# A four-layer convolution and attention network: the gating pass reordered with its norm folded in, and the convolution's scales moved by 0/1 products

## The chip, the cores and the metric

The kernel runs on one core of one Trainium2 chip. The metric is the device time of one execution in microseconds; the kernel before takes 4220.08 us, the median of three runs (4215.15 to 4225.31). Everything is computed in float32.

The profile names the engines so: PE is TensorE (matrix products; PEld its loads of the stationary operand), DVE is VectorE, ACT is ScalarE, POOL is GpSimd, SP is SyncE, which here only issues transfers. Names that end in q are the engines' instruction queues.

## The reference, cut to what matters

The input is x of shape (8, 384, 32, 32). Four layers follow, each with a group norm ahead of it and a residual around it. The change concerns the seam inside layer 0 and the beginning of layer 1.

```python
x = x + L0(gn(x)); x = x + L1(gn(x)); x = x + L2(gn(x)); x = x + L3(gn(x))

def L0(x):        # for each of q, k, v: depthwise 3x3, batch norm over all 8 images, gelu, 1x1
    y = depthwise3x3(x, dw)
    y = gelu((y - mean(y)) * rsqrt(var(y) + 1e-5) * g + b)     # mean, var over images and pixels
    q = einsum('oc,bchw->bohw', pw, y)                         # likewise k, v
    out = softmax(q k^T * scale) v                             # 8 heads of 48
    return batch_norm(einsum('oc,bchw->bohw', w_out, out))

def L1(x):        # 4 experts, the 2 best of each pixel
    scores = softmax(x_flat @ gate_w + gate_b)
    top_v, top_i = top_k(scores, 2); top_w = softmax(top_v)
    present[k, e] = does any pixel of all images choose expert e as its k-th
    coef = einsum('ke,kbhw->ebhw', present, top_w)             # every expert runs on every pixel
    return sum over e of coef[e] * (w2[e] @ relu(w1[e] @ x + b1[e]) + b2[e])

def L2(x):        # depthwise 3x3 and 1x1 with weights rounded to -1, 0, 1 and a scale
def L3(x):        # attention with sampled keys
```

Two things force a barrier over all images: the batch norm of layer 0 needs the statistics of all 8 images before the first Gelu, and `present` needs the routing of all 8 images before the first expert's result.

## The kernel before

An image lies in SBUF as 128 partitions of 3 channels each: `x[b].rearrange("(p c) n -> p c n", c=3)`, so a chunk `c` is 128 x 1024. Layer 0's convolution runs on TensorE in groups of 42 channels (nine groups and a rest of six channels), for q, k and v at once; its results go to the DRAM tensors `raw[v]`, and VectorE takes statistics:

```python
raw = [dram.tile([B, C, N], F32, name=f"raw{v}") for v in range(3)]
work = [(b, g) for b in range(B) for g in range(NGC + 1)]       # the rest group is g = NGC = 9
for n, (b, g) in enumerate(work):
    ...                                                        # matmuls into pk[0], pk[1]
                nc.scalar.copy(y[:, hs], pk[h][: 3 * nch, :])
                nc.vector.bn_stats(cst[: 3 * nch, g, 2 * b + h, :], y[:, hs])
    for v in range(3):
        nc.scalar.dma_start(out=raw[v][b, g * GC : g * GC + nch, :], in_=y[v * nch : (v + 1) * nch, :])

scs, shs = bn_params(cst, NGC + 1, gb0[:, 0, :], gb0[:, 1, :], "qkv")
ssd = dram.tile([2, 3, C], F32, name="ssd")
for k, t in enumerate((scs, shs)):                              # 12 small stores ...
    for v in range(3):
        nc.sync.dma_start(out=ssd[k, v, : NGC * GC]..., in_=t[v * GC : (v + 1) * GC, :NGC])
        nc.scalar.dma_start(out=ssd[k, v, NGC * GC :]..., in_=t[v * GR : (v + 1) * GR, NGC : NGC + 1])
for k, t in enumerate((sc0, sh0)):                              # ... and 6 loads
    for v in range(3):
        nc.sync.dma_start(out=t[:, v * KC : (v + 1) * KC], in_=ssd[k, v].rearrange("(c p) -> p c", p=P))
```

The scales `scs` and shifts `shs` are made in the partitions of the convolution groups and are wanted in the partitions of the activations `g`, which are loaded again from `raw`. Gelu applies them, then the projections run:

```python
nc.scalar.activation(g[:, c, :], g[:, c, :], AF.Gelu, bias=sh0[:, j : j + 1], scale=sc0[:, j : j + 1])
...
load_b(0); gelu_b(0)                                            # gelu_b goes over v in (2, 0, 1)
for v in range(2):
    for h in range(2):
        project(0, 0, v, h)                                     # pq <- w_in[v], g
```

Attention ends with `out_project` (`po`), whose result goes to `o_dram`; a check of the sums decides whether a slower branch runs. It doesn't run here. Then comes what prepares layer 1, in this order:

```python
gw, gbias, ewt = load_w("gw"), load_w("gbias"), load_w("ewt")
w1, b1, w2, b2 = (load_w(n) for n in ("w1", "b1", "w2", "b2"))
...                                                             # dw2, pw2: ternary weights of layer 2, 35 DVE steps
wq3, wk3, wv3, wp3 = (load_w(n) for n in ("wq3", "wk3", "wv3", "wp3"))
...                                                             # small weights of layer 3
xc = pc.enter_context(tc.tile_pool(name="c_x", bufs=2))
for b in range(B):
    load_image(xt, x_img[b]); load_image(ot, o_dram[b])
    for c in range(KC):
        nc.scalar.activation(ot[:, c, :], ot[:, c, :], AF.Identity, bias=..., scale=...)
        nc.vector.tensor_tensor(xt[:, c, :], xt[:, c, :], ot[:, c, :], ALU.add)
        nc.sync.dma_start(out=x1_dram[b][:, c, :], in_=xt[:, c, :])
    ss = gn_stats(xt, f"c{b}", pool=wd)                         # scale and shift of the group norm
    for c in range(KC):
        affine(h1[:, c, :], xt[:, c, :], ss)
    for t in range(NT8):                                        # 8 x 3 matmuls: pixels x experts
        for c in range(KC):
            nc.tensor.matmul(pg[:, t * NE : (t + 1) * NE], lhsT=h1[:, c, t * P : (t + 1) * P],
                             rhs=gw[:, c, :], start=(c == 0), stop=(c == KC - 1))
    ...                                                         # lg = pg + bias; softmax, top 2, pres, wk
```

`gn_stats` is six `bn_stats`, an aggregate, two small matmuls with copies between them (sums over the partitions of a group) and a power on GpSimd. After the loop a matmul joins `pres` over the partitions, and layer 1 proper begins: `layer1(pl, b)` loads `x1_dram[b]` again, normalises it and runs the experts (`ph`, `y`) with results of three PSUM banks. From then on the units of layer 1 of image b+1 are mixed with layers 2 and 3 of image b.

Of the kernel before, what the change touches and what calls it, by code (L numbers as in the profile page):

```python
# [40 lines left out]
def tile_kernel(ctx: ExitStack, tc: tile.TileContext, i: dict, out: bass.AP):  # L41
# [108 lines left out]
    def ternary(dst, w, shape, scale_ap):  # L150

        if isinstance(scale_ap, list):
            for c, s in enumerate(scale_ap):
                nc.vector.tensor_scalar(dst[:, c, :], w[:, c, :], s, RNE, ALU.mult, ALU.add)
        else:
            nc.vector.tensor_scalar(dst, w, scale_ap, RNE, ALU.mult, ALU.add)
        nc.vector.tensor_scalar(dst, dst, RNE, 1.0, ALU.subtract, ALU.min)
        nc.vector.tensor_scalar(dst, dst, -1.0, None, ALU.max)
        nc.vector.tensor_tensor(dst, dst, w, ALU.subtract)
        nc.vector.tensor_tensor(dst, w, dst, ALU.add)  # L160
# [10 lines left out]
    raw = [dram.tile([B, C, N], F32, name=f"raw{v}") for v in range(3)]  # L171
    sc0 = const.tile([P, 9], F32, name="sc0")
    sh0 = const.tile([P, 9], F32, name="sh0")
    with ExitStack() as pa:
# [27 lines left out]
        gb0 = load_a("gb0")  # L202

# [36 lines left out]
        work = [(b, g) for b in range(B) for g in range(NGC + 1)]  # L240
# [7 lines left out]
        for n, (b, g) in enumerate(work):  # L248
            if n + AHEAD < len(work):
                b2, g2 = work[n + AHEAD]  # L250
                if g2 == 0:
                    norm(b2)
                    if b2 + 1 < B:
                        load_x(b2 + 1)
# [24 lines left out]
            for v in range(3):  # L279
                nc.scalar.dma_start(  # L280
                    out=raw[v][b, g * GC : g * GC + nch, :], in_=y[v * nch : (v + 1) * nch, :]
                )

        scs, shs = bn_params(cst, NGC + 1, gb0[:, 0, :], gb0[:, 1, :], "qkv")
        ssd = dram.tile([2, 3, C], F32, name="ssd")
        for k, t in enumerate((scs, shs)):
            for v in range(3):
                nc.sync.dma_start(
                    out=ssd[k, v, : NGC * GC].rearrange("(g c) -> c g", c=GC),
                    in_=t[v * GC : (v + 1) * GC, :NGC],  # L290
                )
                nc.scalar.dma_start(
                    out=ssd[k, v, NGC * GC :].rearrange("(c g) -> c g", g=1),
                    in_=t[v * GR : (v + 1) * GR, NGC : NGC + 1],
                )
        for k, t in enumerate((sc0, sh0)):
            for v in range(3):
                nc.sync.dma_start(
                    out=t[:, v * KC : (v + 1) * KC],
                    in_=ssd[k, v].rearrange("(c p) -> p c", p=P),  # L300
                )
# [28 lines left out]
    def gelu_image(g, v):  # L330
        for c in range(KC):
            j = v * KC + c
            nc.scalar.activation(  # L333
                g[:, c, :], g[:, c, :], AF.Gelu,
                bias=sh0[:, j : j + 1], scale=sc0[:, j : j + 1],
            )

    with ExitStack() as pb:
# [26 lines left out]
        def load_b(b):  # L365
            acts[b] = []
            for v in range(3):
                g = gp.tile([P, KC, N], F32, tag=f"g{v}", name=f"g{v}_{b}", bufs=2 if v < 2 else 1)
                load_image(g, raw[v][b].rearrange("(c p) n -> p c n", p=P))
                acts[b].append(g)  # L370

        def gelu_b(b):
            for v in (2, 0, 1):
                gelu_image(acts[b][v], v)
# [173 lines left out]
    with tc.If(redo > 0):  # L548
        with ExitStack() as pb:
# [13 lines left out]
            with tc.For_i(0, B) as bi:  # L563
                act = []
                for v in range(3):
                    g = gp.tile([P, KC, N], F32, tag=f"g{v}", name=f"g{v}_e")
                    nc.sync.dma_start(
                        out=g, in_=raw[v][bass.ds(bi, 1)].rearrange("o (c p) n -> p (o c) n", p=P)
# [112 lines left out]
    def load_w(name, pool=wd):  # L681
        src = i[name]
        t = pool.tile(list(src.shape), F32, tag=name, name=name + "_sb")
# [4 lines left out]
    w1, b1, w2, b2 = (load_w(n) for n in ("w1", "b1", "w2", "b2"))  # L688


    tap2 = wd.tile([P, KC, 9], F32, name="tap2")
    upw2 = wd.tile([P, KC, C], F32, name="upw2")
    m2 = wd.tile([P, KC], F32, name="m2")
    s2 = wd.tile([P, KC], F32, name="s2")
    with tc.tile_pool(name="w2_raw", bufs=1) as wr:
        dw2 = load_w("dw2", wr)
        pw2 = load_w("pw2", wr)
        nc.vector.tensor_reduce(m2, dw2, AX.X, ALU.add, apply_absolute_value=True)
        nc.vector.tensor_scalar(m2, m2, 1.0 / 9.0, 1e-5, ALU.mult, ALU.max)
        nc.vector.reciprocal(s2, m2)  # L700
        ternary(tap2, dw2, None, [s2[:, c : c + 1] for c in range(KC)])
        nc.vector.reciprocal(m2, s2)
        for c in range(KC):
            nc.vector.tensor_scalar(tap2[:, c, :], tap2[:, c, :], m2[:, c : c + 1], None, ALU.mult)
        mp = wd.tile([P, 1], F32, name="mp")
        sp = wd.tile([P, 1], F32, name="sp")
        nc.vector.tensor_reduce(mp, pw2, AX.XY, ALU.add, apply_absolute_value=True)
        pm = bank("pm")
        nc.tensor.matmul(pm[:, 0:1], lhsT=ones, rhs=mp, start=True, stop=True)
        nc.vector.tensor_scalar(mp, pm[:, 0:1], 1.0 / (C * C), 1e-5, ALU.mult, ALU.max)  # L710
        nc.vector.reciprocal(sp, mp)
        ternary(upw2, pw2, None, sp)
        nc.vector.reciprocal(mp, sp)


    wq3, wk3, wv3, wp3 = (load_w(n) for n in ("wq3", "wk3", "wv3", "wp3"))
    pb3, dw3, bn3, pw3 = (load_w(n) for n in ("pb3", "dw3", "bn3", "pw3"))
    ref3, npos = load_w("ref3"), load_w("npos")
    so3 = wd.tile([P, 1], F32, name="so3")
    bo3 = wd.tile([P, 1], F32, name="bo3")  # L720

    nc.vector.tensor_scalar(bo3, bn3[:, 4:5], 1e-6, None, ALU.add)
    rsqrt(so3, bo3, 1)
    nc.vector.tensor_tensor(so3, so3, bn3[:, 1:2], ALU.mult)
    nc.vector.tensor_tensor(bo3, bn3[:, 0:1], bn3[:, 3:4], ALU.subtract)
    nc.vector.scalar_tensor_tensor(bo3, bo3, so3, bn3[:, 2:3], ALU.mult, ALU.add)

    x1_dram = [dram.tile([P, KC, N], F32, name=f"x1_{b}") for b in range(B)]
    wk = wd.tile([P, B, 2, NT8], F32, name="wk")
    pres = wd.tile([P, 2, NE], F32, name="pres")
    nc.vector.memset(pres, 0.0)
    ss1 = []

    def bc(ap):
        return ap.unsqueeze(2).to_broadcast([P, NT8, NE])

    with ExitStack() as pc:  # L740
        xc = pc.enter_context(tc.tile_pool(name="c_x", bufs=2))
        tcp = pc.enter_context(tc.tile_pool(name="c_t", bufs=2))
        ew_b = ewt.unsqueeze(1).to_broadcast([P, NT8, NE])
        for b in range(B):
            xt = xc.tile([P, KC, N], F32, tag="x", name=f"xc{b}")
            load_image(xt, x_img[b])
            ot = xc.tile([P, KC, N], F32, tag="o", name=f"oc{b}")
            load_image(ot, o_dram[b])
            for c in range(KC):
# [5 lines left out]
                nc.sync.dma_start(out=x1_dram[b][:, c, :], in_=xt[:, c, :])  # L755
            ss = gn_stats(xt, f"c{b}", pool=wd)
            ss1.append(ss)
            h1 = xc.tile([P, KC, N], F32, tag="h", name=f"hc{b}")
            for c in range(KC):
                affine(h1[:, c, :], xt[:, c, :], ss)  # L760
            pg = bank(f"pg{b}")
            for t in range(NT8):
                for c in range(KC):
                    nc.tensor.matmul(
                        pg[:, t * NE : (t + 1) * NE],
                        lhsT=h1[:, c, t * P : (t + 1) * P],
                        rhs=gw[:, c, :],
                        start=(c == 0),
                        stop=(c == KC - 1),
                    )  # L770

            def tt(name):
                return tcp.tile([P, NT8, NE], F32, tag=name, name=f"{name}_{b}")

            def tv(name):
                return tcp.tile([P, NT8], F32, tag=name, name=f"{name}_{b}")

            lg, e, sc, eq, oh = tt("lg"), tt("e"), tt("sc"), tt("eq"), tt("oh")
            m, d = tv("m"), tv("d")
            nc.vector.tensor_tensor(  # L780
                lg, pg[:, : NT8 * NE].rearrange("p (t e) -> p t e", e=NE),
                gbias.unsqueeze(1).to_broadcast([P, NT8, NE]), ALU.add,
            )
            nc.vector.reduce_max(m, lg, AX.X)
            nc.vector.tensor_tensor(lg, lg, bc(m), ALU.subtract)
            nc.scalar.activation(e, lg, AF.Exp)
            nc.vector.reduce_sum(m, e, AX.X)
            nc.vector.reciprocal(m, m)
            nc.vector.tensor_tensor(sc, e, bc(m), ALU.mult)
            tops = []  # L790
            for k in range(2):
                mk, ek, hit = tv(f"m{k}"), tv(f"e{k}"), tcp.tile(
                    [P, NE], F32, tag=f"hit{k}", name=f"hit{k}_{b}"
                )
# [3 lines left out]
                nc.vector.tensor_tensor(eq, eq, ew_b, ALU.mult)  # L798
# [7 lines left out]
            nc.vector.tensor_tensor(d, tops[1], tops[0], ALU.subtract)  # L806
            nc.scalar.activation(d, d, AF.Exp)
            nc.vector.tensor_scalar(m, d, 1.0, None, ALU.add)
            nc.vector.reciprocal(wk[:, b, 0, :], m)
            nc.vector.tensor_tensor(wk[:, b, 1, :], d, wk[:, b, 0, :], ALU.mult)  # L810
# [17 lines left out]
    for k, t in enumerate((dp, p1)):  # L828
        nc.vector.tensor_tensor(ybt, b2, t.unsqueeze(1).to_broadcast([P, KC, NE]), ALU.mult)
        nc.vector.reduce_sum(yb[:, k, :], ybt, AX.X)  # L830

# [38 lines left out]
    def layer1(pl, b):  # L870
# [5 lines left out]
        def enter(h):  # L876
# [6 lines left out]
            for t in range(4):  # L883
                w0 = wk[:, b, 0, 4 * h + t : 4 * h + t + 1].to_broadcast([P, P])
                nc.tensor.matmul(
                    pw[:, t * P : (t + 1) * P], lhsT=w0, rhs=ident, start=True, stop=True
# [368 lines left out]
    with ExitStack() as pd:  # L1255
        pl = Pools(pd, "d", 5)
        for u in layer1(pl, 0):
            u()
        for b in range(B):
# [57 lines left out]
def _layouts(a):  # L1317
# [33 lines left out]

    hrow = np.arange(C).reshape(NH0, HD0)
# [6 lines left out]
    for n in "qk":  # L1359
        L[f"w{n}0"] = _chunks(a[f"L0_conv_pw_{n}"].T[order][:, rows])  # L1360
# [56 lines left out]
```

## Time and profile before

| what | value |
|---|---|
| median of 3 runs | 4220.08 us (4215.15 to 4225.31) |
| span of the profiled run | 4222.7 us |
| PE, share of the span | 3887.0 us, 92% |
| DVE | 1624.3 us, 38% |
| ACT | 1512.2 us, 36% |
| POOL | 261.5 us, 6% |
| moved by DMA | 238.60 MB, mean 57 GB/s |

The profile is of one execution. The page gives the busy time of each engine, the span in 40 equal slices, the costliest groups of instructions and the transfers. Further views answer for a stretch of time: busy times in given stretches, who waited for whom, and the instructions in order of time. In a line of a group, the words are the line of the program, the engine, the operation, output and inputs by the program's names, the shape, the count, busy time and mean, then the idle time ahead of it and what ended that. Ends of matmuls are modelled, so a busy PE is not PE at its peak; and the page's share of busy time is a mean over stages that have different limits.

### The profile page before, as it was taken

What the parts mean: (1) busy time and instruction counts of PE and PEld (TensorE: products, weight loads), DVE (VectorE), ACT (ScalarE), POOL (GpSimd) and SP (SyncE); (2) the same over time, 40 slices, a digit from 0 to 9 for tenths busy, and PEclk for the clock granted to TensorE, in tenths of its full rate; (3) what the DMA queues carried; (4) which work ended last, traced back from release to release, by engine and by line L of the source; (5) the groups of instructions that cost most, each with busy time, mean ns of one, the idle gap of its engine ahead of it and who ended that gap; (6) DMA issues with size and microseconds to landing.
All of it is one profiled execution on the core that took longest, in us unless ns stands there. A gap on an engine that the chain in (4) does not pass through costs nothing.

```text
span 4222.7 us, 31867 instructions
## 1 busy us (share of the span) xinstructions
PE 3887.0 (92%) x11992; PEld 1647.5 (39%) x11992; DVE 1624.3 (38%) x2807; ACT 1512.2 (36%) x1683; POOL 261.5 (6%) x157
## 2 busy tenths in 40 slices
PE   7999699999999999999347999999999999999957
PEld 3444233333333333333244444444445354444423
DVE  3333111121211111221343373836465655737364
ACT  2222364546364554334122223232423232232313
POOL 0000000000000000000000002020201111020202
PEclk9999899999999999999557999999999999999978
DMA  6776411111111010000542000000000000000000
GB/s 200 216 214 199 130 50 29 43 37 50 30 44 54 22 50 24 18 19 10 219 179 85 0 16 30 15 15 30 15 30 15 15 15 30 15 30 15 1 30 16
DMA packets 81554, 238.60 MB, mean 57 GB/s; under 512 B 20830, under 2 KB 21214, under 8 KB 81006
## 3 DMA queue, kind: packets, MB, share of 16 engines
q1 hardware_dynamic: 68932, 198.67, 14.4%
q10 hardware_dynamic: 12456, 37.76, 2.9%
q8 instruction: 99, 1.62, 0.2%
q14 instruction: 67, 0.55, 0.0%
HBM read 100.50 MB, written 88.09 MB: 45 GB/s over the span
## 4 chain that ended last, share of the span: by engine, by line


## 5 line engine op out<-in xcount | busy, mean ns | idle before, releaser
L458 ACT ACTIVATE p<-s 128x1024 f32<-128x1024 f32 x512 | 497.6, 1021 | 653.2 <-PE s L451 652.5
L923 PE MATMUL y<-hd,w_sb 128*128 128x512 f32 x1152 | 523.7, 598 | 0.0
L903 PE MATMUL ph<-h,w_sb 128*128 128x512 f32 x1152 | 503.0, 595 | 0.0
L464 PE MATMUL pav<-p,vt 128*64 128x512 f32 x2048 | 499.2, 608 | 0.0
L451 PE MATMUL s<-qk,qk 48*128 48x512 f32 x1536 | 383.8, 618 | 22.2 <-ACT p L458 22.2
L271 PE MATMUL pk<-st,cw_sb 126*126 126x496 f32 (+1 forms) x864 | 383.2, 606 | 0.8 <-DVE ve_a L111 0.8
L903 PEld LDWEIGHTS ph<-h,w_sb 128*128 128x128 f32 x1152 | 217.9, 191 | 262.9 <-issue 257.5
L923 PEld LDWEIGHTS y<-hd,w_sb 128*128 128x128 f32 x1152 | 212.0, 190 | 260.4 <-issue 248.5
L464 PEld LDWEIGHTS pav<-p,vt 128*64 128x64 f32 x2048 | 124.8, 136 | 342.7 <-issue 334.1
L271 PEld LDWEIGHTS pk<-st,cw_sb 126*126 126x126 f32 x864 | 167.6, 196 | 211.7 <-issue 205.0
L431 DVE STREAM_TRANSPOSE tu<-pav 128x512 f32<-128x512 f32 x64 | 45.9, 717 | 503.5 <-PE pav L464 503.5
L973 DVE SCALAR_TENSOR_TENSOR y<-h,tap,y 128x961 f32<-128x961 f32 (+1 forms) x192 | 231.8, 1232 | 1.8
L1053 DVE SCALAR_TENSOR_TENSOR off<-q,dw_sb,off 128x240 f32<-128x240 f32 (+2 forms) x576 | 230.2, 459 | 2.6
L913 ACT ACTIVATE hd<-ph,b_sb 128x512 f32<-128x512 f32 x192 | 131.2, 683 | 278.4 <-PE ph L903 278.2
L451 PEld LDWEIGHTS s<-qk,qk 48*128 48x128 f32 x1536 | 131.2, 186 | 253.6 <-issue 173.2
L278 DVE BATCH_NORM_STATS2 cst<-y 126x6 f32<-126x512 f32 (+1 forms) x160 | 109.0, 690 | 252.2 <-ACT y L277 252.1
L277 ACT COPY y<-pk 126x512 f32<-126x512 f32 (+1 forms) x160 | 92.9, 584 | 287.5 <-PE pk L271 192.8
L914 DVE TENSOR_TENSOR hd<-hd,cb 128x512 f32<-128x512 f32 x192 | 132.1, 688 | 118.6 <-ACT hd L913 118.2
L400 PE MATMUL pq<-g,wq_sb 128*128 128x512 f32 x288 | 138.4, 617 | 34.3 <-ACT g L333 34.3
L126 ACT ACTIVATE h<-x,ss_d 128x1024 f32<-128x1024 f32 x48 | 56.8, 1231 | 298.3 <-DVE ss_d L114 298.3
L984 PE MATMUL pw<-y,upw 128*128 128x512 f32 x288 | 132.3, 615 | 31.2 <-DVE y L973 31.2
L1143 ACT ACTIVATE p<-s 128x1024 f32<-128x1024 f32 x96 | 93.6, 1020 | 173.0 <-PE s L1136 172.9
(218 smaller groups left out, 4113.3 us busy)
## 6 DMA issues: line engine op xcount, KB each, us to landing
g<-raw SPq DMA_DIRECT2D x72, 512.0 KB
st<-pad SPq DMA_DIRECT2D x216, 168.0 KB
raw<-y ACTq DMA_DIRECT2D x216, 168.0 KB
x<-x SPq DMA_DIRECT2D x48, 512.0 KB
xa<-in_x_dram SPq DMA_DIRECT2D x24, 512.0 KB
o<-ot SPq DMA_DIRECT2D x48, 256.0 KB
xc<-in_x_dram SPq DMA_DIRECT2D x24, 512.0 KB
oc<-o SPq DMA_DIRECT2D x24, 512.0 KB
```

The costliest lines, as they stand in the source:

```text
L271: nc.tensor.matmul(pk[h].rearrange("p (h w) -> p h w", w=W)[: 3 * nch, :, o0 : o0 + c1 - c0], lhsT=lhs, rhs=rhs, start=(k == 0), stop=(k = ...
L400: nc.tensor.matmul(pq, lhsT=w_in[v][:, c, pr * P : (pr + 1) * P], rhs=acts[b][v][:, c, h * HALF : (h + 1) * HALF], start=(c == 0), stop=(c ...
L451: nc.tensor.matmul(s[:, j * HALF : (j + 1) * HALF], lhsT=kt[r, kc * P : (kc + 1) * P], rhs=qt[r, h * HALF : (h + 1) * HALF], start=True, s ...
L458: nc.scalar.activation(p, s, AF.Exp, scale=scale)
L464: nc.tensor.matmul(pav[64 * j : 64 * j + 64, :], lhsT=vts[b % 2][:, kc, 2 * hd : 2 * hd + 2, :].rearrange("p a b -> p (a b)"), rhs=p[:, j ...
L903: nc.tensor.matmul(ph, lhsT=w1[:, e, c, dc * P : (dc + 1) * P], rhs=state["h1"][:, c, :], start=(c == 0), stop=(c == KC - 1),)
L913: nc.scalar.activation(hd, ph, AF.Relu, bias=b1[:, k : k + 1])
L914: nc.vector.tensor_tensor(hd, hd, state["cb"], ALU.mult)
L923: nc.tensor.matmul(y, lhsT=w2[:, e, dc, m * P : (m + 1) * P], rhs=state[k], start=(k == 0), stop=(k == NE * KC - 1),)
L973: nc.vector.scalar_tensor_tensor(d, src[:, r0 + dy : r1 + dy, c0 + dx : c1 + dx], tap2[:, c, t : t + 1], d, ALU.mult, ALU.add,)
L984: nc.tensor.matmul(pw[:, hs], lhsT=upw2[:, c, m * P : (m + 1) * P], rhs=y[:, c, hs], start=(c == 0), stop=(c == KC - 1),)
L1053: nc.vector.scalar_tensor_tensor(d, f, dw3[:, t : t + 1], d, ALU.mult, ALU.add)
```

## The change

It joins two changes that stand side by side.

The first concerns the gating pass. Images are loaded ahead of the weights, in four buffers and not two, and the group norm in front of the gate is folded into the gate's weights: with scale a and shift s per channel, `gate_w . (a x + s)` is `(a gate_w) . x + s . gate_w`. So the normalised image is not made; the gate weights are the stationary operand and the image streams past them, 512 pixels at a time; the logits come out with experts in the partitions and are transposed back by four small matmuls. Routing runs twice (after images 0 to 5 and 6, 7) and not once an image. The x1 stores are issued by ScalarE's queue. The ternary weights of layer 2 are prepared later, within layer 1 of image 0 (`weights23`).

The second concerns the scales of the convolution. `raw` is laid out as the images are, so that a channel's partition is given by three blocks of 42 and a rest of two, and the scales reach it through products with 0/1 matrices (`sel0`, `sel1`) and a mask, with no trip to DRAM. The rest group comes first in each image. Gelu goes over q, k, v, and the rows of the projection weights follow the new channel order.

```diff
-    raw = [dram.tile([B, C, N], F32, name=f"raw{v}") for v in range(3)]
+    raw = [dram.tile([B, P, KC, N], F32, name=f"raw{v}") for v in range(3)]
-        work = [(b, g) for b in range(B) for g in range(NGC + 1)]
+        work = [(b, g) for b in range(B) for g in (NGC, *range(NGC))]
 ...
-        ssd = dram.tile([2, 3, C], F32, name="ssd")
-        (12 stores to ssd, 6 loads from it)
+        nc.vector.tensor_copy(both[:, 0, :], scs)
+        nc.vector.tensor_copy(both[:, 1, :], shs)
+        nc.vector.tensor_tensor(rest, both[: 3 * GR, :, NGC:]..., one3..., ALU.mult)
+        for v in range(3):
+            nc.tensor.matmul(pm[:, 0, v, : 2 * (NGC + 1)], lhsT=sel0[:, v, :], rhs=both..., ...)
+            nc.tensor.matmul(pm[:, 1, v, : 2 * KC], lhsT=sel1[:, v, :], rhs=rest..., ...)
+        for v in range(3):
+            nc.vector.tensor_tensor(got[:, v], pm[:, 0, v, ...]..., msk..., ALU.mult)
+        nc.vector.reduce_sum(ss0..., got..., AX.X)
+        nc.vector.tensor_tensor(ss0..., ss0..., pm[:, 1, :3, : 2 * KC], ALU.add)
 ...
-            for v in (2, 0, 1):
+            for v in (0, 1, 2):
                 gelu_image(acts[b][v], v)
 ...
-    w1, b1, w2, b2 = (load_w(n) for n in ("w1", "b1", "w2", "b2"))
-    (ternary weights of layer 2, weights of layer 3)
-        xc = pc.enter_context(tc.tile_pool(name="c_x", bufs=2))
+        xc = pc.enter_context(tc.tile_pool(name="c_x", bufs=4))
 ...
-                nc.sync.dma_start(out=x1_dram[b][:, c, :], in_=xt[:, c, :])
+                nc.scalar.dma_start(out=x1_dram[b][:, c, :], in_=xt[:, c, :])
-            (affine of three chunks; 24 matmuls pg with the image stationary)
+            nc.vector.tensor_scalar(gwa, gw, ss[:, 0:1], None, ALU.mult)
             for c in range(KC):
+                for h in range(2):
+                    nc.tensor.matmul(pl[32 * h : 32 * h + NE, :], lhsT=gwa[:, c, :],
+                                     rhs=xt[:, c, h * HALF : (h + 1) * HALF], ...)
+            nc.tensor.matmul(pt[:, :NE], lhsT=ss[:, 1:2].to_broadcast([P, P]), rhs=gws, ...)
+            nc.vector.tensor_tensor(gb, pt[:, :NE], gbias, ALU.add)
+            (2 copies pl -> ls, 4 transposes ls -> pt, 2 adds of gb into lg)
 ...
+        for b in range(4):
+            load_c(b)
+        w1, b1 = load_w("w1"), load_w("b1")
+        for b in range(B):
+            if b == 2:
+                w2, b2 = load_w("w2"), load_w("b2")
+            residual(b)
+            if b + 4 < B:
+                load_c(b + 4)
+            if b == 5:
+                route(0, 6)
+        (weights of layer 3)
+        route(6, B)
 ...
-        for u in layer1(pl, 0):
+        for k, u in enumerate(layer1(pl, 0)):
             u()
+            if k == 12:
+                tap2, upw2, mp, so3, bo3 = weights23(pl)
```

## The prediction

> **What bounds the kernel now.** I read the 40 slices first, then the busy times of the stretches between the stages, then the waits, last the timeline at the two seams.
>
> The slices of the page (one digit is a tenth of busy time in 105.6 us, PEclk the granted TensorE clock in tenths):
> ```profile
> PE   7999699999999999999347999999999999999957
> PEclk9999899999999999999557999999999999999978
> DMA  6776411111111010000542000000000000000000
> ```
> TensorE is at 9 nearly everywhere, so the kernel is bound by its matmuls, except in slices 19 to 21 (about 2006 to 2320 us): there PE falls to 3 and 4, its clock to one half, and the DMA engines are only half busy. That is the gating pass. A dent in slice 4 (PE 6) is the seam between convolution and attention.
>
> The stretches, cut at the first and last matmuls of the neighbours (columns: stretch, length, busy us and instructions of PE, PEld, DVE, ACT, POOL, then granted clock, DMA share, GB/s):
> ```profile
> 450.60:484.70 34.10, 0.01 (x1) 0.05 (x1) 2.89 (x8) 3.21 (x4) 9.39 (x5) 0.51 0.72 161
> 484.70:2025.40 1540.70, 1513.90 (x5346) 522.74 (x5346) 286.71 (x466) 760.83 (x748) 0.00 (x0) 0.99 0.12 38
> 2025.40:2058.10 32.70, 0.56 (x2) 0.50 (x2) 12.40 (x35) 0.00 (x0) 0.85 (x1) 0.55 0.67 261
> 2058.10:2267.10 209.00, 95.03 (x416) 91.73 (x416) 82.83 (x300) 58.35 (x62) 4.96 (x9) 0.50 0.49 181
> ```
> Attention (second line) is 98% PE and can't give much. The other three lines hold 34.1 + 32.7 + 209.0 us in which no engine is near full. With the 7.5 us up to the first expert matmul at 2274.6, the gating part lasts 249.2 us.
>
> The waits say what stands there. PE's waits at the seam, then PE's and DVE's in the gating part (engine, line, what ended the wait: total, times, longest):
> ```profile
> PE pq L400 <- ACT g L333: 34.1, 1, 34.1
> ...
> PE pm L709 <- DMA wk_sb<-in_wk_dram: 26.6, 1, 26.6
> ...
> DVE lg L780 <- PE pg L764: 104.9, 8, 13.2
> ```
> At the seam, the first projection waits 34.1 us for the first Gelu, which itself waits (the waits of ACT: `sh<-ssd`, 24.9 us) for scales that go to DRAM and back. In the gating part, PE first waits 26.6 us for weights; then DVE waits 13.1 us in each of 8 images for the gate matmuls. Their group:
> ```profile
> L764 PE MATMUL pg<-gw_sb,hc 128*128 128x4 f32 x384 | 85.8, 355 | 27.9 <-ACT hc L126 27.9
> ```
> Its 85.8 us over 8 images are 10.7 each, in 48 records, two to an f32 matmul: 24 matmuls of which each loads 128x128 of data as weights in order to make four columns. The image loop is a serial ring: gate matmuls 11.1, routing mixed with the next residual 8.6, norm chain 3.3, first affine 1.3, together the 25.1 us from one `lg` to the next that the timeline shows (2091.1, 2116.1).
>
> **What the skill says.** "TensorE: Matmul & The Clock Gate", What's actually happening: the clock is gated to half when PE has been idle; agrees, 0.50 granted from 2058 on. So I price gating matmuls at half clock. "DMA: Bandwidth & Descriptors", Specifications: about 358 GB/s from HBM for a core. This trace does better: 407 GB/s at a share of 0.99 from 2041 to 2051 us, for pure weight loads; the measurement decides, but reads mixed with writes I put at 350. Same page, Issuing engines are not separate DMA queues: moving the x1 writes to ScalarE's queue buys issue time, not bandwidth. "ScalarE: Activation LUTs", What ACT_TABLE_LOAD costs: about 1283 ns; the trace has 1283 ns.
>
> **Part A, the scales of the convolution.** Removed: twelve stores to DRAM and six loads back, with the queue waits around them. Added: two copies, one product, six matmuls against 0/1 tables, three masked products, a sum and an add. Path after the last conv matmul at 450.6, with durations of this trace: ScalarE copy 0.7, bn_stats 0.7, aggregate 0.6, eps 0.2, POOL power 2.2 with its gap, three small DVE steps 0.6 (to here it is the old path, without the 6.2 us by which the last small group's copy came late), copies and product 0.6, six narrow matmuls, 12 records at the 0.23 of the gate's (11.1 / 48), 2.8, five small DVE steps 1.0, table load 1.5, first Gelu 1.3: 12.2 us, so 463. The rest group now comes first in each image, so that 18-row work does not end the stage. But the data must be there too: the SP queue issues seven `g` loads from 450.6 to 459.3, and wq0 after them. 7 x 0.52 + 0.59 = 4.3 MB at 350 GB/s is 12 us, plus 2 for completion: 465. So the transfers, not the scales, end last; PE starts at about 466 and not at 484.7. **Gain 18 us.** The new Gelu order (0, 1, 2) and the row order of weights change no count; the first PE wait already ended on a q Gelu. I take 0.
>
> **Part B, the gating pass.** What it must move: 24 x 3 transfers of 524 KB = 37.7 MB, w1 and w2 4.7, the later weights 2.9, x1 of image 0 again 1.6: 46.9 MB, 134 us at 350 GB/s. Per image, the engines:
> - DVE: three adds (1.1 apart) and six bn_stats (0.62 apart) 7.1; norm chain 1.2; gate weights, bias, two logit copies of 0.65, two adds 2.2: 10.5 us.
> - PE: 6 matmuls 512 wide, 12 records of 0.85 at half clock (the spacing of the `po` records after 2010). The two halves write different rows of the bank, as the `pav` pairs do, whose 8 records take 1.94 us at full clock, half of their single cost; so 5.1. Transposes and small ones 3. Some 8 us.
> - ACT: three affines 3.7; the three of the normalised image (28.0 / 8 = 3.5) vanish.
> - Routing: twice in place of eight times, 25 short DVE instructions of 0.2 to 0.25: 6 each.
>
> DVE 8 x 10.5 + 12 = 96 us, PE 64, ACT 30, DMA 134: **the pass turns from a ring of latencies into a DMA stage**. Its length: 7.6 us from the last matmul to the first image load (redo branch and small loads, as 2025.4 to 2033 now); then what must land ahead of image 7's compute, 46.9 less later weights, the last two x1 writes and the reload (2.9 + 3.1 + 1.6), 39.3 MB, 112 us; 2 completion; the tail of image 7: affine, add, stats 3.7, norm 3.5, gate weights and matmuls 5.4, copies 1.3, transposes and adds 2.6, 16.5; last routing 5.5; presence 2. Sum 145.6. I add 10 for starts and queue waits that don't overlap: 156. **Gain 249.2 - 156 = 93 us.** Of this, 27 us are the weights and the ternary ahead of the first image.
>
> **Part C, what is given back.** The ternary of layer 2 moves into layer 1 of image 0: about 12 us of DVE. There DVE is idle 8.9 us at a time while `y` matmuls run, but they share three banks with `pm`. I take 2 us of PE stall. Tables (0.22 MB) and a rest group that needs all three padded chunks at the start: 1 us.
>
> Sum: 4220 - 18 - 93 + 3 = **4112 us**.
>
> **Rivals.**
> 1. *The ring stays, with another link.* If DVE's order puts image b's logit copies before image b+1's adds, each image pays 10.5 + 5.1 (matmuls) + 2 (transposes) + 2 (norm waits) = 19.6 us, the pass 8 x 19.6 + 12 + 20 = 189, the gain 60: 4145. For it: engines run in order. Against: the trace now mixes `m`, `sc`, `eq` of one image with adds and stats of the next, so the compiled order does interleave.
> 2. *The writes on ScalarE's queue hold ScalarE up.* At 450.3 to 456.5 a ScalarE copy sat 6.2 us behind its queue's issues, and the wait was ended by `DMA g<-raw`, a load of the other queue. With 24 or more loads queued, a write might wait for many of them, and ScalarE's next affine with it. Cost 10 to 30 us: 4120 to 4140.
> 3. *Full rate.* Transfers at 407 GB/s and all compute under them: the pass is about 137 us, the gain 112: 4093.
> 4. *The values come late.* With v's Gelu last, `pv` could stall PE in every image. Against: PE waits only 22 us for Exp in the whole stage, and has other work. Up to 20 us worse.
>
> **Range and chances.** Part B carries the doubt: gain 60 to 112; Part A 12 to 22. Ends added: 4089 to 4151; widened a little, 4085 to 4152. Faster by 2% means below 4135.7, a total gain of 84: only rival 1, or rival 2 with a weak Part A, misses it. Faster 0.83, within 2% 0.16, slower 0.01: no part adds PE work of size to the stages that PE bounds.
>
> **What will show it.** Right: PE's wait at the seam 15 to 18 us, ended by a DMA or a Gelu whose input came late; the stretch from the last `po` matmul to the first `ph` about 156 us with a DMA share of 0.85 or more; no wait of DVE for a gate matmul over 6 us; expert stage within 3 us of 1948. Wrong: a share near 0.6 with DVE waiting on `pl` (rival 1), ACT idle until `DMA x<-xc` or `xc<-in_x_dram` (rival 2), new PE waits in attention on `pv` (rival 4), or a PE wait on `y` or `pm` of over 5 us in the first layer 1 (Part C).

## The result, and the profile after

The changed kernel takes 4107.52 us (4102.84 to 4114.03), the kernel before 4221.88 us in the runs beside it: a ratio of 0.973, 95% interval 0.971 to 0.975, so 2.7% faster. The prediction was 4112.0.

The slices of the changed kernel's page, each now 102.6 us long:
```profile
PE   7999899999999999999649999999999999999947
...
PEclk9999999999999999999869999999999999999978
DMA  6777411111110111000380000000000000000000
```
Where PE stood at 3, 4, 7 in slices 19 to 21, it stands at 6, 4, 9: the hole is narrower, not gone. In it the DMA engines now reach 8 in place of 5. The dent of slice 4 went from 6 to 8.

The same stretches as before, from the view of busy times by stretch (length, busy us and instructions of PE, PEld, DVE, ACT, POOL, granted clock, DMA share, GB/s). The borders are: end of the last convolution matmul, first projection, last matmul of attention, first image load, then two parts of the gating loop:
```profile
445.60:463.40 17.80, 3.30 (x14) 3.08 (x13) 3.05 (x14) 5.90 (x6) 6.04 (x3) 0.60 0.91 331
463.40:2009.50 1546.10, 1522.31 (x5346) 524.12 (x5346) 286.61 (x465) 758.62 (x746) 3.37 (x3) 0.99 0.12 37
2009.50:2017.50 8.00, 0.09 (x1) 0.01 (x1) 2.90 (x6) 0.00 (x0) 0.98 (x2) 0.69 0.13 43
2017.50:2125.00 107.50, 40.93 (x134) 14.12 (x134) 72.25 (x154) 28.54 (x24) 4.16 (x7) 0.60 0.96 375
2125.00:2150.00 25.00, 12.07 (x42) 3.98 (x42) 15.77 (x52) 1.74 (x3) 1.65 (x3) 0.64 0.64 231
```
The seam is 17.8 us and was 34.1. Attention is 1546.1 us and was 1540.7, which nobody asked for. The gating part, with the 6.7 us from 2150.0 to the first expert matmul at 2156.7, is 147.1 us and was 249.2. In the 107.5 us where images flow in, the DMA engines are busy at 0.96 and move 375 GB/s. That line looks like a stage bound by transfers. The experiments say otherwise.

At the seam, the waits of all engines (engine, line, what ended the wait: total, times, longest):
```profile
PE pmove L299 <- DVE both L291: 9.6, 1, 9.6
ACT y L277 <- DMA g<-raw: 6.4, 1, 6.4
...
PE pq L419 <- DMA wq_sb<-in_wq_dram: 4.9, 1, 4.9
```
PE's one wait of 34.1 us has become two, 9.6 for the scales and 4.9 for the first projection's weights; between them stand the 0/1 products. What the weights themselves waited for stands in SyncE's queue. Its wait at the seam, then the last instructions of the scales, the load and the first Gelu in order of time (start, us, engine, line):
```profile
SPq L369 <- DVE ss L315: 5.1, 1, 5.1
```
```profile
458.91 0.21 DVE L315 TENSOR_REDUCE ss<-got 128x18 f32<-128x54 f32 x1
459.15 0.17 DVE L318 TENSOR_TENSOR ss<-ss,pmove 128x18 f32<-128x18 f32 x1
459.19 0.33 SPq L369 DMA_DIRECT2D wq_sb<-in_wq_dram  x1
...
459.36 6.90 ACT L352 ACTIVATE g<-g,ss 128x1024 f32<-128x1024 f32 x6 [5.61 <-DVE ss L318]
```
The load of `wq` is issued only when the sum of the scales is done (L315, until 459.12), and 4.2 us later PE starts. So the load that PE waits for last stands itself behind the scales. (L315 is the last reader of `got`, whose pool closes there; that the weights take over its memory would explain the wait, but no run tests it.)

In the gating part, VectorE's waits:
```profile
DVE ls L761 <- PE pl L748: 16.5, 5, 5.2
DVE gb L758 <- PE plt L754: 6.5, 3, 2.7
DVE xc L737 <- DMA xc<-in_x_dram: 4.7, 2, 3.1
...
DVE ve_c L111 <- PE gnb_c L109: 3.9, 6, 0.7
DVE ss_c L114 <- POOL ss_c L85: 3.5, 5, 0.8
DVE ga_c L103 <- PE gna_c L101: 2.8, 4, 0.7
...
DVE xc L737 <- ACT oc L733: 1.3, 2, 1.1
```
The 104.9 us for gate matmuls (eight waits of 13.1) have become 16.5 in five. And of the stops in this list, only 4.7 + 1.3 us end with something that was loaded (the 1.3 by way of ScalarE); the other 33.2 us are round trips of VectorE's own results through TensorE or GpSimd. From the first residual add to the last logits:
```profile
2023.00:2149.30 126.30, 53.00 (x176) 18.09 (x176) 86.92 (x197) 28.79 (x25) 4.95 (x9) 0.61 0.90 351
```
86.9 us are work and 39.4 are stops. That the two fill the stretch is so for any engine; what tells is what ended the stops: 33.1 us are the round trips above, 1.6 a load (the other wait for a load, 3.1 us, lies ahead of the first add), 1.3 ScalarE, and the rest are stops of under 1 us each. So the 147.1 us are 13.5 before the first add, VectorE's 126.3, and 7.4 from the last logits to the first expert matmul.

The gate's group, from the groups of the gating stretch, against 85.8 us in 384 records before:
```profile
L748 PE MATMUL pl<-xc,gwa 128*4 128x512 f32 x96 | 37.4, 944 | 11.0 <-DVE gwa L744 8.2 <-DMA xc<-in_x_dram 1.5 <-DVE bo L894 1.2
```
37.4 / 8 = 4.7 us an image, where it was 10.7.

### The profile page after: what moved, and what is told of

Its sections match the earlier page's. It is cut to its first block, busy times and chain, and to the rows that moved or that the text cites. A ratio compares the mean times of both kernels' runs of the same rounds, so it can differ in the third digit from the quotient of the medians.

```text
span 4104.3 us, 31246 instructions
## 1 busy us (share of the span) xinstructions
PE 3847.9 (94%) x11764; PEld 1576.4 (38%) x11764; DVE 1629.1 (40%) x2710; ACT 1482.8 (36%) x1647; POOL 262.4 (6%) x159
## 4 chain that ended last, share of the span: by engine, by line
## 5 line engine op out<-in xcount | busy, mean ns | idle before, releaser
L271 PE MATMUL pk<-st,cw_sb 126*126 126x496 f32 (+1 forms) x864 | 374.0, 595 | 0.8 <-DVE ve_a L111 0.8
L66 DVE COPY qk<-pq 128x512 f32<-128x512 f32 x48 | 33.2, 692 | 300.4 <-PE pq L419 201.4
```

What stands on the lines that cost most here:

```text
L271: nc.tensor.matmul(pk[h].rearrange("p (h w) -> p h w", w=W)[: 3 * nch, :, o0 : o0 + c1 - c0], lhsT=lhs, rhs=rhs, start=(k == 0), stop=(k = ...
```

## The experiments

Medians are of four timed executions unless said otherwise, and those of one kernel spread over some 2 to 11 us; a difference of 5 us between two medians is at the edge of what they can tell. The stages are from the one profiled execution of each kernel. Two kernels with the same gating code (the changed one, and the one of the Gelu order below) had 147.1 and 150.5 us there, so under 4 us a stage tells nothing either.

### Each half alone

The gating half alone (convolution, its scales, Gelu order and weights' rows as before):

> The kernel before with the gating part of the change alone; the scales still go through DRAM. Theory (the two parts add, because each fills its own stretch in which TensorE has nothing to do): gating stretch about 147 us as in the changed kernel, seam 34 us as before, so 4222 - 102 = 4120 us, within 5. Rival (the seam's 16 us are given back later, as the 5 us longer attention stage of the changed kernel hints): about the same as the changed kernel, 4108 us.

4121.33 us, ratio 0.977 (0.975 to 0.979). Its gating part is 147.0 us, its seam 34.2, its attention 1539.0.

The scales half alone (gating as before):

> The kernel before with the scales part of the change alone. Theory: seam from 34 to about 18 us, gating stretch 249 us as before: 4222 - 16 = 4206 us, ratio 0.996. Rival (order of groups and of Gelu cost attention what the seam gains): 4222 us, ratio 1.000. Rival (the 5 us by which the convolution ended earlier belong to the change, not to the granted clock): 4200 us.

4212.05 us, ratio 0.9986 (0.9979 to 0.9993; 20 executions). Its seam is 18.4 us, its gating part 249.6, its attention 1546.1. So the seam gave 15.7 us, and attention took 5.4 back. In the profiled executions the two halves add up (103.3 + 15.9 us against 118.4 for both). In medians they are 96.3 + 5.6 us, both against 4217.63 us, the median of 23 executions of the kernel before; the changed kernel, timed apart, lies 110.1 us below the same figure. The difference is one of the executions that were profiled: that of the kernel before took 4224.54 us, 6.9 above this median, and that of the scales half 4208.61, 3.4 below its own. So the scales half is worth some 6 us, not the 16 of its seam. The 8 us by which the joined kernel beats the sum of its halves are as much as its interval allows (0.002 of the time); the rest stays open.

### Order and buffers, or the folded norm

The changed kernel with the normalised image made again, in one buffer, and the 24 gate matmuls of four columns, all else as changed:

```diff
-            (gwa; 6 matmuls pl of 512 pixels each; plt, ls, transposes)
+            for c in range(KC):
+                affine(h1[:, c, :], xt[:, c, :], ss)
+            for t in range(NT8):
+                for c in range(KC):
+                    nc.tensor.matmul(pg[:, t * NE : (t + 1) * NE],
+                                     lhsT=h1[:, c, t * P : (t + 1) * P], rhs=gw[:, c, :], ...)
```

> The changed kernel with the old gate: the image is normalised by ScalarE (one buffer) and is the stationary operand of 24 matmuls of four columns, as before; order of loads, four buffers, two routings, late ternary as in the changed kernel. Theory (load order and buffering make the gain, the stage is bound by transfers of about 14 us an image, and 24 matmuls are 11 us of TensorE): gating stretch 150 to 165 us, total 4110 to 4125 us. Rival (the folded norm makes the gain; with one h buffer the ring affine, gate, norm of 25 us per image stays): 20 to 25 us an image, stretch 200 to 225 us, total 4160 to 4185 us.

4157.79 us, ratio 0.986 (0.984 to 0.987). The gating part is 195.4 us. So of the 102.1 us that it lost, 53.8 belong to the order, the buffers, the queue of the stores and the routing done twice, which no run takes apart, and 48.3 to the fold. Of these, up to 10.6 may belong to the single buffer, as the kernel before had two: ScalarE waited once, 10.6 us, until TensorE had read the buffer. VectorE's largest wait in this kernel:
```profile
DVE lg L757 <- PE pg L750: 87.5, 8, 13.3
```
The ring is there again: eight waits of 10.9 us for the gate matmuls. Images ahead of the weights and four buffers alone don't open it.

### Are the transfers the limit?

With a DMA share of 0.96, I took transfers away. The x1 stores (24 of 524 KB, 12.6 MB) are left out, and layer 1 loads the input image in their place, which leaves out layer 0's residual from there on:

```diff
-                nc.scalar.dma_start(out=x1_dram[b][:, c, :], in_=xt[:, c, :])
...
-        load_image(xt, x1_dram[b])
+        load_image(xt, x_img[b])
```

> The changed kernel without the stores of x1 (12.6 MB); layer 1 loads the input image instead, so the output leaves out layer 0's residual from layer 1 on. Theory (transfers set the length of the gating stretch, 0.90 of the DMA engines at 348 GB/s): 12.6 MB less at 348 GB/s are up to 36 us, of which the last two images' stores (3.1 MB, 9 us) lie behind the last load: 20 to 30 us less, 4078 to 4088 us, until VectorE's 96 us become the bound. Rival (VectorE's order and the norm chain set it): under 8 us less, about 4100 us.

4105.48 us, ratio 0.973 (0.971 to 0.975), and a gating part of 147.5 us: nothing gained. From first add to last logits:
```profile
2028.80:2154.90 126.10, 53.69 (x176) 17.92 (x176) 86.55 (x197) 28.59 (x25) 5.88 (x9) 0.61 0.62 251
```
The DMA share fell from 0.90 to 0.62, the issue of the last image load ended 31 us earlier (2088.7, not 2119.9), VectorE waited for no load in it, and the stretch is the same to 0.2 us. **The transfers nearly fill the time that VectorE's order takes; they don't set it.**

### Is VectorE's work the limit?

The statistics of each chunk are taken a second time into a tile that nobody reads, 48 more `bn_stats`:

```diff
                 st = gn_start(xt, f"c{b}", c, st)
+                sx = gn_start(xt, f"cx{b}", c, None if c == 0 else sx)
```

> The changed kernel with six more bn_stats per image in the gating pass, whose results nobody reads: 48 x 0.62 = 30 us more on VectorE, no byte more. Leaving out 12.6 MB of stores gained nothing, so the theory that transfers alone set the gating stretch has fallen. Theory 2 (the order on VectorE sets it: adds and statistics, then a stop of up to 5 us for the gate's matmuls): 20 to 30 us longer, 4128 to 4138 us. Rival (transfers set it after all, and the run without stores had another limit): under 8 us longer, 4108 to 4115 us. In between: both limits lie close together.

4118.34 us, ratio 0.976 (0.974 to 0.978): some 11 us slower. The stretch from first add to last logits, and two of VectorE's waits in the gating part:
```profile
2028.10:2161.20 133.10, 53.83 (x176) 18.35 (x176) 112.57 (x245) 28.69 (x25) 4.95 (x9) 0.60 0.84 331
```
```profile
DVE gb L759 <- PE plt L755: 9.6, 7, 2.4
DVE ls L762 <- PE pl L749: 4.9, 1, 4.9
```
25.7 us more work made the stretch 6.8 us longer; the stops fell from 39.4 to 20.5 us, the waits for `pl` from 16.5 to 4.9. The time came out between the two expectations, where two limits close together would put it; but VectorE's waits for loads are 1.8 us here, so no transfer took over: the new work went into the stops. So VectorE's busy time alone doesn't set the stretch, nor do the transfers; its order with the round trips in it does: of work that comes while a round trip is under way, about a quarter showed.

Then what of work that stands where no round trip is? The routing of images 0 to 5 does. In the changed kernel's order of time it lies between 2115.8 and 2132.1 us, mixed with the adds and statistics of images 6 and 7, and from 2112.9 to 2132.1 VectorE never stops for longer than 0.42 us. Here it is left out, on top of the stores (a constant takes the place of those images' weights):

```diff
+    nc.vector.memset(w0, 0.5)
...
-            if b == 5:
-                route(0, 6)
```

> As the run without the x1 stores (4105.5 us, gating pass 147.5 us), and in addition the routing of images 0 to 5 is left out (a constant takes the place of their weights); the routing of 6 and 7 stays. With the stores gone, the DMA engines have room (share 0.76). Theory V (VectorE's work in order is the limit then): the 25 or so routing instructions of some 0.3 us, 8 us in all, stand in front of the last two images' adds, so the pass falls to 138 to 141 us and the time to 4096 to 4099. Theory L (the loads alone, or the fixed head and tail, are the limit): the pass stays at 146 to 148, the time at 4104 to 4107.

```profile
2027.10:2147.60 120.50, 52.10 (x176) 17.75 (x176) 81.27 (x174) 28.52 (x23) 5.89 (x9) 0.63 0.65 265
```
Against the run without the stores, VectorE's work is 5.3 us less and the stretch 5.6 us shorter: one for one, if this one pair of profiles is taken as it stands (5.6 is little above the 4 us within which a stage tells nothing). The gating part is 141.3 us. The expected 138 to 141 took the routing for 8 us. The time, 4103.81 us (0.973; 0.971 to 0.975), moved by only 1.7, within the spread of the medians, as this execution's attention was 1549.6 us.

### Moving the routing

If the end of VectorE's order counts, routing belongs earlier. Images 0 to 2 are routed after image 3, and 3 to 7 at the end, in a kernel that has two other edits besides (the next section's), so it is read against that one:

```diff
-            if b == 5:
-                route(0, 6)
+            if b == 3:
+                route(0, 3)
...
-        route(6, B)
+        route(3, B)
```

> As the run with both (old Gelu order, last stores on SyncE), with the routing split otherwise: images 0 to 2 after image 3, images 3 to 7 at the end, in place of 0 to 5 after image 5 and 6, 7 at the end. Theory V (VectorE near the end of the pass counts, its middle does not): the 9 us of routing between 2115 and 2132 us move to where the transfers set the pace, and the last routing grows by some 3 us: the pass falls by 3 to 6 us, the time likewise. Theory L (loads set the pace to the end): the pass grows by the 3 us of the larger last routing.

The stretch from first add to last logits is 123.8 us, 2.5 shorter than its neighbour's, which is less than a stage's scatter; from the last logits to the first expert matmul it is 10.5 us and not 7.4. The gating part, 147.0 us, is what it was: what the earlier routing may have given, the last one took back. The time was 4114.59 us (0.976; 0.974 to 0.978), against 4109.81 for its neighbour: nothing gained.

### Filling the stops, and fewer buffers

Image b's adds and statistics are put ahead of image b-1's gate, so that a round trip of one runs under the work of the other; routing becomes 0 to 3 and 4 to 7:

```diff
             residual(b)
+            if b > 1:
+                gate_out(b - 2)
+            if b > 0:
+                gate_in(b - 1)
+                if b + 3 < B:
+                    load_c(b + 3)
+            if b == 6:
+                route(0, 4)
```

> The changed kernel with the gate of image b behind the adds of image b+1 (norm and gate matmuls) and of b+2 (copies and transposes), and routing split 4 and 4 and not 6 and 2. Same work, same bytes. Theory (two limits of about equal length, VectorE's order and the transfers at a share of 0.96): VectorE's stops of 16.5 us for the gate's matmuls and 6.5 us for the shift's go away, but the transfers stay, so only the end of the pass gets shorter: 4 to 12 us less, 4096 to 4104 us. Rival (VectorE's order alone): 20 to 25 us less, 4083 to 4088 us. Rival (the compiled order hardly follows the program's): 4108 us.

4112.66 us (0.975; 0.973 to 0.977), gating part 147.9. No gain. The same without the x1 stores, so that no transfer could hide one:

> The same reordering without the stores of x1 (layer 1 loads the input image; layer 0's residual is left out from layer 1 on). Theory (two limits): with both lowered, the pass gets shorter by 20 to 30 us than in the changed kernel, 4078 to 4088 us, although leaving out the stores alone gained nothing. Rival (a third limit, such as the pace of the queue's issues or the tail of the last image): within 8 us of the kernel with the reordering alone.

4104.71 us (0.973; 0.971 to 0.974), gating part 144.7, where a fall of 20 us or more was expected. The stops are still there. VectorE's waits in this kernel, then three of its instructions in order of time:
```profile
DVE ls L771 <- PE pl L753: 20.4, 7, 5.4
...
DVE xc L738 <- ACT oc L734: 3.7, 1, 3.7
```
```profile
2070.30 0.23 DVE L749 TENSOR_SCALAR gwa<-gw_sb,ss_c 128x12 f32<-128x12 f32 x1
2070.44 0.31 DVE L99 BATCH_NORM_AGGREGATE mv_c<-st_c 128x2 f32<-128x36 f32 x1
2075.14 0.68 DVE L771 COPY ls<-pl 4x512 f32<-4x512 f32 x1 [4.39 <-PE pl L753]
```
Here an image's copies `ls` still follow its gate weights `gwa` with no add or statistic of another image between them. The waits for `pl` are 20.4 us in seven, against 16.5 in five in the changed kernel: the order that was compiled is not the one that was written. (ScalarE stood 25.6 us ahead of the first routing's Exp, but VectorE waited for ScalarE only once, 3.7 us, ahead of the first add.) So what filled stops would be worth isn't known; no run here had that order.

Two image buffers in place of four:

```diff
-        xc = pc.enter_context(tc.tile_pool(name="c_x", bufs=4))
+        xc = pc.enter_context(tc.tile_pool(name="c_x", bufs=2))
...
-        for b in range(4):
+        for b in range(2):
```

> The changed kernel with two and not four image buffers, two images loaded ahead. Theory 2 (VectorE's order sets the pass): the loads of image b+2 wait for the gate matmuls of image b and then take 8 us, so a part of the DMA time comes out from under VectorE's: 10 to 25 us longer, 4118 to 4133 us. Rival (depth doesn't matter, only that images come ahead of weights): 4108 us within 4.

4112.01 us (0.975; 0.973 to 0.976), gating part 152.8. The two further buffers are worth 4.5 us in the median and 5.7 in the stage, both at the edge of what can be told.

### Attention and the seam

Attention became 5.5 us longer in the changed kernel, and it is between 1546.1 and 1550.7 us in every kernel that has the scales half, against 1540.7 and 1539.0 in the two that don't. The first suspicion was the order of the Gelus. The old one again, for images 1 to 7:

```diff
-            for v in (0, 1, 2):
+            for v in (0, 1, 2) if b == 0 else (2, 0, 1):
```

> The changed kernel with the Gelu order of before (2, 0, 1) for images 1 to 7; image 0 keeps 0, 1, 2. Theory O (the order of the Gelus costs the attention stage its 6 to 10 us): the stage returns from 1546-1550 us to 1540-1542, the time to 4100 to 4102. Theory C (it is the granted clock, or the table load that now stands elsewhere, whatever the order): stage 1546 to 1550, time 4106 to 4109.

Attention stayed at 1547.7 us, the time at 4108.11 us (0.974; 0.972 to 0.975). It isn't the order. What differs is the clock. The second 64.4 us of attention in the kernel before, then in the changed one:
```profile
549.10:613.50 64.40, 58.88 (x215) 18.96 (x214) 9.75 (x16) 45.76 (x43) 0.00 (x0) 0.97 0.17 55
```
```profile
527.80:592.20 64.40, 60.17 (x206) 18.63 (x204) 8.85 (x16) 45.33 (x42) 0.00 (x0) 0.92 0.18 55
```
PE does nine fewer matmuls in 1.3 us more of busy time, at a granted clock of 0.92 and not 0.97. With attention divided into 24 equal parts, the sum of length times (1 - granted clock) is 10.9 and 12.8 us in the two kernels without the scales half, and 15.5 to 20.7 in the ten others that were divided so; PE's idle time is 23 to 30 us over both groups. (The view gives the clock to 0.01, which can move such a sum by 1 to 2 us, so the gap between the groups is thin.) In the changed kernel the clock covers the loss: 17.4 us against 10.9, where attention is 5.5 longer; in the one with the old Gelu order it covers part of it, 15.5 us against 10.9 for 7.0. Why the clock falls more often there isn't shown.

Last, the seam. The raw stores of the last image's last groups go to SyncE, so that ScalarE's copy no longer sits behind them for 6.4 us (together with the old Gelu order):

```diff
-                nc.scalar.dma_start(out=to, in_=y[v * nch : (v + 1) * nch, :])
+                (nc.sync if b == B - 1 and 5 <= g < NGC else nc.scalar).dma_start(
+                    out=to, in_=y[v * nch : (v + 1) * nch, :]
+                )
```

> The run with the old Gelu order, and in addition the raw stores of the last image's last four small groups issued from SyncE and not from ScalarE, whose queue held a copy up by 6.4 us at the seam. Theory S (the held ScalarE copy delays the scales, and these the first Gelu): seam 17.7 -> 12 to 14 us, time 4 to 6 us under the run with the old Gelu order. Theory T (the loads of g and then of the first projection's weights end last, as the prediction had it): seam 17 to 19, time within 2 us of that run.

4109.81 us (0.975; 0.973 to 0.976); the seam is 21.5 us, not shorter. ScalarE's wait, and SyncE's issues in order of time:
```profile
ACT L354 <- DMA g<-raw: 18.2, 1, 18.2
```
```profile
451.83 0.37 SPq L371 DMA_DIRECT2D wq_sb<-in_wq_dram  x1
...
453.66 8.17 SPq L145 DMA_DIRECT2D g<-raw  x9
```
The scales were there at 451.97, 7.4 us earlier than the 459.32 of the changed kernel, and with them the load of `wq`, which again waited for their sum (SyncE's wait for `ss` at L317: 7.0 us). But here the loads of `g` stand behind the weights in SyncE's queue, so they were issued only from 453.66, and not from 445.65, and ScalarE waited for them until 461.6. So the run traded one wait for another and doesn't test the scales alone: what earlier scales with the loads of `g` where they were would bring stays open.

None of these kernels beats the changed one by more than the spread of the medians.

## Why the prediction was right, and where its reasons were not

| part | predicted | measured, profiled executions |
|---|---|---|
| seam | -18 | -16.4 |
| gating | -93 | -102.1 |
| expert stage, tables, padding | +3 | -0.5 (expert stage alone: 1947.6 against 1948.1) |
| convolution | 0 | -5.0 |
| attention | 0 | +5.5 |
| sum | -108 | -118.4 |

**The sum.** That 4112.0 lies within 5 us of 4107.52 is in part luck. Timed by halves, the gating half gave 96 us where 93 were predicted, and the scales half 6 where 18 were. In the profile, too, errors of both signs meet.

**Part A.** The seam's gain was right within 2 us, its reason was not. The step that fails is "the transfers, not the scales, end last". PE's last wait (4.9 us) does end with a transfer, that of `wq`, but SyncE held this transfer back for 5.1 us until the scales were summed, and the first Gelu waited for the scales as well. So the scales' path sets the seam, and it was mis-sized: by the prediction's sum the first Gelu should have begun 10.9 us after the last convolution matmul (12.2 less its own 1.3), and it began 13.8 us after it (459.36 against 445.6), although the table load no longer stood on the path (it ran at 452.47, before the scales came). ScalarE's copy sat 6.4 us behind `g<-raw`: the same wait of 6 us that the prediction had taken off because the rest group now comes first. It moved from that small group to a large one. Of the 17.8 us, 13.6 are this path up to the issue of `wq` and 4.2 the load behind it; the prediction had 14 us of loads from the end of the convolution on, and the scales beside them. That both give about the same gain is luck. The sign to look for was one wait of 15 to 18 us; two came, 9.6 and 4.9.

**Part B, the amounts.** From the last matmul of attention to the first of the experts:
```profile
2009.50:2156.70 147.20, 55.58 (x188) 20.49 (x189) 96.37 (x237) 32.72 (x31) 6.79 (x12) 0.60 0.86 334
```
VectorE's work was put at 96 us and is 96.4, of which 2.9 lie ahead of the images; ACT at 30 and is 32.7; PE at 64 and is 55.6. The gate matmuls, 5.1 us an image, are 4.7; pairs of halves in different rows do overlap as was read from `pav`. The four links of the old ring add up to 24.3 us, not to the 25.1 that stands beside them.

**Part B, the cause.** The step that fails is "the pass turns from a ring of latencies into a DMA stage". Its signs came as written (share 0.86, length 147.1 for 156, longest gate wait 5.2), and yet 12.6 MB less moved nothing. The length 156 was a sum of transfers, a tail for image 7 and an allowance of 10 us for queue waits; the true length is 86.9 us of VectorE's work with 39.4 of stops, 13.5 before and 7.4 after. That the two come within 9 us of each other is luck, since leaving out 12.6 MB would have shortened the first by up to 36 us and left the second as it is. The rate of 350 GB/s was also too low: 375 with the stores in between, and many of the 2.4 us slices of the view of transfers, from 2025 to 2120 us, at 410 to 425. The Trainium skill has this in "HBM Reference", Specifications (TRN2): a core that streams alone measures about 425 GB/s, above its share of 358; the slices agree. And "Perfetto Trace Analysis", Identifying the Most-Contended Engine, calls occupancy misleading for DMA; this case agrees, with a share of 0.96 that was no limit. The rate of transfer, which that section puts in its place, would have misled as well: 375 of some 425 GB/s.

**The rivals.** Rival 1 (the ring stays) is the nearest in mechanism: VectorE's order does set the pace, but with stops of 39.4 us in eight images and not the 9 us in each that the rival assumed; 147 us, not 189. Rival 2 didn't come: VectorE waited for ScalarE only 1.3 us in all. Rival 3, full rate with all compute under it, has the nearest number of the rivals (137), not the cause; the terms that the prediction lists give 130 at 407 GB/s, so where its 137 comes from can't be seen. Rival 4 fell: PE's list of waits in attention has no `pv`.

**Part C.** 3 us were set and none was found: from 2150 to 2500 us PE has no wait on `y` or `pm`. So the ternary of layer 2 cost PE no wait that shows.

**The zeros.** Two stages that were given 0 moved by 5 us each and cancelled, which is luck. The convolution ended between 442.7 and 450.2 us in kernels that have the same convolution code up to its last image, so its 5 us are in part chance. Attention's are not, as all kernels with the scales half agree, and they cost a third of what the seam gave or more (5.4 to 10.0 us).

## What to carry to other kernels

A DMA share near 1 in a stage doesn't make it a DMA stage when buffers let the loads run ahead: look at the engine that the images pass through in order, and see what ended its stops (here 33.1 of 39.4 us its own round trips, 1.6 a load); then take transfers away. On such an engine, ask of each piece of work whether it falls into a round trip's wait (25.7 us more cost 6.8) or stands where no wait is (5.3 us less gave 5.6). A last wait that ends with a load says little until you have seen what that load waited for in its queue. When work is reordered in the program, check in the trace that the stops went: here they stayed, 20.4 us for `pl` against 16.5.

## What the runs showed of the hardware that was not expected

With the same 5346 matmul records and about the same idle time, attention lost more to the granted clock in the kernels with the scales half (15.5 us or more, against 12.8 or less). The clock fell for a few us at a time, and with PE at work all through: in the changed kernel it is 0.50 from 568.7 to 572.0 and from 578.9 to 585.6 us, where PE is busy for all of the 3.3 and 6.7 us. A ScalarE instruction behind its own queue's store issues was held for 6.4 us, and the event that freed it belongs to a load that SyncE had issued, in the changed kernel as in the one before (6.2 us): the second store of the three was issued at 443.56, the third at 449.74.
